# A narrower source for each packed tile's gather in a stack of four sparse graph attention layers

## The chip, the cores and the metric

The kernel runs on one core of one Trainium2 chip, as one launch. The metric is the device time of a launch in microseconds (us). TensorE (PE) multiplies matrices, VectorE (DVE) and ScalarE (ACT) do the elementwise work, GpSimd (POOL) issues the indirect DMAs, and SyncE (SP) issues the direct ones. Each engine works through its own queue in order; a semaphore makes an instruction wait for another engine or for a DMA.

## The reference, cut to what matters

There are 4096 nodes of 256 features and an adjacency matrix in which about one entry in 256 is set, besides the diagonal. Four graph attention layers follow one another, each with a residual and a layer norm:

```python
x = _layernorm(x + _L0_gnn_ref(x, adj, ...))   # 4 heads of 64
x = _layernorm(x + _L1_gnn_ref(x, adj, ...))   # 4 heads of 64
x = _layernorm(x + _L2_gnn_ref(x, adj, ...))   # 2 heads of 128
x = _layernorm(x + _L3_gnn_ref(x, adj, ...))   # 1 head, positive and negative attention
# within a layer, with h the projected nodes:
e = leaky_relu(s_src[i] + s_dst[j], 0.2)       # only where adj[i, j] is set
out[i] = sum_j softmax_j(e)[i, j] * h[j]
```

The sum over j has non-zero terms only for the neighbours of i.

## The kernel before, in words

**Packing.** The 4096 nodes are 32 row tiles of 128. The rows i of one tile m together have neighbours among some 40% of all nodes, so the kernel doesn't go through all 32 column tiles. It packs the nodes j that any row of tile m needs into 13 packed tiles of 128 (NG = 13, L71), in rising order of j. The tile's own 128 nodes come in addition, unpacked, as the seventh of 14 positions (FRONT = 6, L78; NP, L72). Nodes of the first 17 column tiles (MIX, L77) are laid from the front, the others from the back end. `windows()` (L101-122) computes, from the mean and 4.5 standard deviations of the number of touched nodes, which packed tiles a column tile j can reach: WINDOW[m, j] is a first packed tile and a number. If a node falls outside of that, a flag is set and a dense program computes everything (L165-168); with these inputs it isn't entered.

`Program.lists` (L285-475) makes the lists, while layer 0 already runs: `prepare` reads the adjacency (4 MB per block of four row tiles) and makes bytes of it, `places` computes each node's place, and `pack` (L416-451) moves, by one-hot matmuls (L436), the masks and the node numbers to their places. L448 to L451 compose the node number of each packed place from three digits, clip it, and write it to `idx[:, m, t]`: 128 node numbers of packed tile t of row tile m.

**Layers.** `Projection` (L520-591) computes, for one row tile of the next layer, the rows that the neighbours will need (values of all heads and attention terms) and stores them to DRAM as 128 rows of `vals` (L574). Each layer has a `vals` of its own with 4096 rows. `RowTile.load` (L614-631) fetches what one row tile of a layer needs, in two halves of seven positions: the own rows by a direct DMA (L626), each of the 13 packed tiles by an indirect DMA on POOL (L629), which takes 128 rows of `vals` by the numbers in `idx`. The buffers of these rows (`G`) come from a pool of 16 slots, two positions to a slot (one in layer 3, whose second halves have 14 slots of their own). `RowTile.half` (L633-682) then computes the attention weights `w` on ACT (L670, L657) and DVE (L666, L667, L671) and multiplies on PE (L679, L682). In layers 2 and 3 the last 3 and 1 blocks of four row tiles are computed unpacked, over all 32 column tiles (`whole_rows`, L866-919; PE L911).

**Order.** The order is written out by hand: `run` (L478-517), `Layer.part`, `half_alone`, `half_with_whole` and `close` (L744-863). A layer loads the first halves of its tiles 0 to 3 while the one before ends, and then the second half of tile 0. The waits aren't written out: the framework makes a gather wait for those stores whose rows lie in the slice of `vals` that the gather names as its source. L79 sets that slice: for the first six packed tiles (t below FRONT) it is the first 17 x 128 rows, for the other seven it is all 4096.

Of the kernel before, what the change touches and what calls it, by code (L numbers as in the profile page):

```python
# [37 lines left out]
F32 = mybir.dt.float32  # L38
# [7 lines left out]
ALU = mybir.AluOpType  # L46
# [4 lines left out]
P = 128  # L51
N = 4096
# [18 lines left out]
NG = 13  # L71
# [4 lines left out]
LEAD = 10  # L76
MIX = 17  # L77
FRONT = 6  # L78
NODES = tuple(MIX * P if t < FRONT else N for t in range(NG))  # L79
MC = P + 4  # L80
EDGE = 64.0
HEADS = (4, 4, 2, 2)
# [18 lines left out]
def windows():  # L101

    share = 1.0 - (1.0 - 1.0 / 256.0) ** P
    mean, sd = P * share, (P * share * (1.0 - share)) ** 0.5
    dev = 4.5
    out = {}
    for m in range(NT):
        for j in range(NT):
            if j == m:
                continue  # L110
            if j < MIX:
                n = sum(q != m for q in range(j))
                lo = mean * n - dev * sd * n ** 0.5
                hi = mean * (n + 1) + dev * sd * (n + 1) ** 0.5
            else:
                n = sum(q != m for q in range(j, NT))
                lo = CAP - mean * n - dev * sd * n ** 0.5
                hi = CAP - mean * (n - 1) + dev * sd * (n - 1) ** 0.5
            a = max(0, int(lo // P))
            b = min(NG - 1, int((hi - 1) // P))  # L120
            out[m, j] = (a, b - a + 1)
    return out


WINDOW = windows()
assert all(a >= FRONT for (m, j), (a, _) in WINDOW.items() if j >= MIX)
WMAX = max(n for _, n in WINDOW.values()) * P


# [57 lines left out]
class Program:  # L187
# [97 lines left out]
    def lists(self, ctx):  # L285


        tc, nc, ins, shared = self.tc, self.nc, self.ins, self.shared

        def pool(name, bufs):  # L290
            return ctx.enter_context(tc.tile_pool(name=name, bufs=bufs))

        cst, rawp, mkp, ohp = pool("icst", 1), pool("raw", 4), pool("imk", 2), pool("oh", 8)
        wk, cmp_ = pool("iwk", 2), pool("cm", 3)


        iotaI = wk.tile([P, WMAX], I32, name="iotaI", bufs=1)
        nc.gpsimd.iota(iotaI, pattern=[[1, WMAX]], base=1, channel_multiplier=0)
        iota = cst.tile([P, WMAX], F16, name="iota")
        nc.vector.tensor_copy(iota, iotaI)  # L300
# [39 lines left out]
        for j in range(NT):  # L340
            m = 0
            while m < NT:
                if m == j:
                    m += 1
                    continue
                e = m
                while e < NT and e != j and WINDOW[e, j] == WINDOW[m, j]:
                    e += 1
                a, n = WINDOW[m, j]
                nc.gpsimd.memset(lo[:, m:e, j], a * P - 1.0 - (CAP if j >= MIX else 0))  # L350
                nc.gpsimd.memset(wid[:, m:e, j], float(n * P))
                m = e
        total = cst.tile([P, NT], F32, name="total")
        bad = cst.tile([P, BT, NT], F32, name="bad")
        nc.vector.memset(bad, 0.0)

        class Block:
# [58 lines left out]
            def pack(self, it):  # L416
                m, mk = self.blk * BT + it, self.mk
                cm = cmp_.tile([P, NP, P], U8, name="cm")
                nc.scalar.copy(cm[:, FRONT, :], mk[:, m, it, :P])
                order = [j for j in range(NT) if j != m]  # L420
                touches = {}
                for j in order:
                    a, n = WINDOW[m, j]
                    for k in range(a, a + n):
                        touches.setdefault(k // 3, []).append((j, k))
                accs = {}
                for j in order:
                    a, n = WINDOW[m, j]
                    oh = ohp.tile([P, WMAX], BF16, name="oh")
                    nc.vector.tensor_scalar(oh[:, :n * P], iota[:, :n * P], self.place[:, it, j:j + 1], None,  # L430
                                            op0=ALU.is_equal)
                    for k in range(a, a + n):
                        b, s = divmod(k, 3)
                        if b not in accs:
                            accs[b] = prog.bank(prog.pfour)
                        nc.tensor.matmul(accs[b][:, s * MC:(s + 1) * MC], oh[:, (k - a) * P:(k - a + 1) * P],  # L436
                                         mk[:, j, it, :].bitcast(FP8), start=touches[b][0] == (j, k),
                                         stop=touches[b][-1] == (j, k), skip_group_check=True)
                        if touches[b][-1] == (j, k):
                            e = min(3, NG - 3 * b)  # L440
                            got = accs[b][:, :e * MC].rearrange("p (s c) -> p s c", c=MC)
                            o = 3 * b + (3 * b >= FRONT)
                            nc.scalar.activation(cm[:, o:o + e, :], got[:, :, :P], AF.Copy, scale=EDGE / 2.0)  # L443
                            nc.scalar.copy(self.num[:, it, 3 * b:3 * b + e, :], got[:, :, P:])
                nc.sync.dma_start(out=shared["maskC"][m], in_=cm)
                num = self.num[:, it]
                t = wk.tile([P, NG], F32, name="t")
                nc.vector.scalar_tensor_tensor(t, num[:, :, 0], 16.0, num[:, :, 1], op0=ALU.mult, op1=ALU.add)  # L448
                nc.vector.scalar_tensor_tensor(t, t, 16.0, num[:, :, 2], op0=ALU.mult, op1=ALU.add)
                nc.vector.tensor_scalar(shared["idx"][:, m, :FRONT], t[:, :FRONT], float(MIX * P - 1), None, op0=ALU.min)  # L450
                nc.vector.tensor_scalar(shared["idx"][:, m, FRONT:], t[:, FRONT:], float(N - 1), None, op0=ALU.min)  # L451

        prog = self
        block = Block(0)
# [23 lines left out]
    def run(self):  # L478
# [3 lines left out]
        with ExitStack() as ctx:  # L482
            lists = self.lists(ctx)
            xs = []
            for q in range(NT // 2):
                slot = self.g0.tile([P, 2 * ROW[0]], F32, name="G")
                nc.sync.dma_start(out=slot[:, :2 * F].rearrange("p (t f) -> p t f", t=2),
                                  in_=to_tiles(ins["x"][2 * q * P:2 * (q + 1) * P, :]))
                xs += [slot[:, :F], slot[:, F:2 * F]]

            line = [Projection(self, 0, w0, x, m, (self.ptwo[0], self.ptwo[1], self.pfour))
                    for m, x in enumerate(xs)]
            turns, listed = NT + 5, 0
            for m in range(turns):
                while listed < BT + LEAD and listed * turns <= m * (BT + LEAD):
                    next(lists)
                    listed += 1
                for k, step in enumerate(Projection.STEPS):
                    if 0 <= m - k < NT:
                        step(line[m - k])  # L500

            for m in range(NT):
                layer.part(m, 0)
                if m + LEAD < NT:
                    next(lists)
                layer.part(m, 1)
            for _ in lists:
                pass
# [11 lines left out]
class Projection:  # L520
# [68 lines left out]
    def all(self):  # L589
        for step in self.STEPS:  # L590
            step(self)


class RowTile:
# [19 lines left out]
    def load(self, half):  # L614
        L, m, n = self.layer, self.m, self.layer.n
        prog, nc, sh = L.prog, L.nc, L.shared
        if half == 0:
            self.S = prog.ld.tile([P, H4, P], F32, name="S")
            nc.sync.dma_start(out=self.S[:, :TERMS[n]], in_=sh["e"][n][m].partition_broadcast(P))
            self.mk = prog.ld.tile([P, NP, P], U8, name="mk")  # L620
            nc.sync.dma_start(out=self.mk, in_=sh["maskC"][m])
        else:
            self.y = L.load_x(m)
        for pos in range(HALF * half, HALF * (half + 1)):
            if pos == FRONT:
                nc.sync.dma_start(out=self.place(pos), in_=sh["v"][n][m * P:(m + 1) * P, :])  # L626
                continue
            t = pos - (pos > FRONT)
            nc.gpsimd.indirect_dma_start(  # L629
                out=self.place(pos), out_offset=None, in_=sh["v"][n][:NODES[t], :],  # L630
                in_offset=bass.IndirectOffsetOnAxis(ap=sh["idx"][:, m, t:t + 1], axis=0))

    def half(self, half):  # L633
# [824 lines left out]
```

## Time and profile before

The median of three runs is 2346.93 us (2338.59 to 2347.44). The profiled execution spans 2346.8 us, at a mean granted TensorE clock of 0.950.

| engine | busy us | share of span | instructions |
|---|---|---|---|
| PE | 2052.4 | 87% | 15689 |
| DVE | 1838.1 | 78% | 6100 |
| ACT | 1747.3 | 74% | 5137 |
| POOL | 1582.6 | 67% | 1596 |

Busy time is a sum over stages that are bound differently, so the shares alone don't tell what the end waits for. The chain of work that ended last is 47% PE, 20% DVE, 18% DMA and 8% ACT; its largest lines are PE L679 (17%) and L682 (12%) and the landing of gathers (12%). By the gathers, layer 0 runs from 101 us (first gather) to 812, layer 1 to about 1350, layer 2 to about 1780 and layer 3 to the end. In the lines of the profile, "G<-vals,idx" is a gather, "vals<-row" the store of a tile of rows, and the bracket at the end of a timeline line gives the idle time ahead of an instruction and the event that ended it, as far as the profile can infer it.

### The profile page before, as it was taken

The numbers are of one execution on the slowest core, as the hardware profiler recorded it, in microseconds if no ns is written. First come the engines' busy times: TensorE is split into PE (matmuls) and PEld (weight loads), VectorE is DVE, ScalarE is ACT, GpSimd is POOL, SyncE is SP. The second block draws the span as 40 slices with busy tenths as digits, with TensorE's granted clock in tenths as the row PEclk, the third lists the DMA queues.
The fourth block names the chain that finished last, engine by engine and source line by source line (L and its number), as shares of the span: only waits on it lengthen the run. The fifth ranks groups of instructions, "written<-read, shape, count | busy, mean of one in ns | idle before, by whom it ended". The sixth has DMA issues, their size and how long they took to land.

```text
span 2346.8 us, 49828 instructions
## 1 busy us (share of the span) xinstructions
PE 2052.4 (87%) x15689; PEld 1864.7 (79%) x15689; DVE 1838.1 (78%) x6100; ACT 1747.3 (74%) x5137; POOL 1582.6 (67%) x1596
## 2 busy tenths in 40 slices
PE   4878898989988769999999889889898799979996
PEld 3668788888888759988888879888887688868885
DVE  3889999999987759989899859876866365656567
ACT  4779898897787749988888859877663666666663
POOL 2127887777788757777777767755553677777773
PEclk7999999999999979999999989999999899989998
DMA  8889687775555556666666657666665788888883
GB/s 278 267 269 322 220 284 255 245 268 155 157 140 159 148 168 182 190 176 170 174 175 183 167 147 202 200 187 188 187 179 150 248 250 276 268 245 267 272 251 119
DMA packets 250325, 492.01 MB, mean 210 GB/s; under 512 B 44385, under 2 KB 156610, under 8 KB 249666
## 3 DMA queue, kind: packets, MB, share of 16 engines
q0 software_dynamic: 81536, 245.30, 37.1%
q1 hardware_dynamic: 168514, 243.42, 32.5%
q8 instruction: 126, 2.06, 0.4%
q14 instruction: 149, 1.22, 0.2%
HBM read 436.24 MB, written 52.31 MB: 208 GB/s over the span
## 4 chain that ended last, share of the span: by engine, by line
PE 47%; DVE 20%; DMA 18%; ACT 8%; issue 4%; POOL 3%; SPq 0%; ACTq 0%; DVEq 0%; POOLq 0%
PE bank L679 17%; PE bank L682 12%; DMA G<-vals,idx 12%; PE bank L911 7%; PE bank L546 5%; DVE w L671 5%; PE bank L436 4%; DMA G<-vals 3%; POOL G L629 3%; DVE w L666 3%; DVE w L667 3%; ACT w L670 3%; DVE oh L430 2%; DMA raw<-in_adjB_dram 2%; ACT pw L900 1%
## 5 line engine op out<-in xcount | busy, mean ns | idle before, releaser
L629 POOL DMA_INDIRECT G<-vals,idx x1456 | 1569.6, 1078 | 718.5 <-issue 188.1
L670 ACT ACTIVATE w<-S,G 128x128 f32<-128x128 f32 x3248 | 1009.6, 391 | 204.7 <-DMA G<-vals,idx 194.6
L679 PE MATMUL bank<-w,G 128*65 128x128 f32 x7168 | 846.8, 279 | 94.9 <-DVE w L667 65.0
L679 PEld LDWEIGHTS bank<-w,G 128*65 128x65 f32 x7168 | 810.4, 142 | 109.8 <-DVE w L667 84.5
L682 PE MATMUL bank<-G,w 128*128 128x257 f32 (+1 forms) x2688 | 499.4, 344 | 34.8 <-ACT z L970 11.5
L682 PEld LDWEIGHTS bank<-G,w 128*128 128x128 f32 x2688 | 439.2, 196 | 84.7 <-ACT z L970 13.9
L671 DVE SCALAR_TENSOR_TENSOR w<-w,mk 128x896 f32<-128x896 f32 x272 | 292.6, 1082 | 42.8 <-ACT w L670 42.1
L911 PE MATMUL bank<-vw,pw 128*128 128x129 f32 (+1 forms) x2048 | 304.8, 306 | 14.3 <-ACT zw L970 13.0
L911 PEld LDWEIGHTS bank<-vw,pw 128*128 128x128 f32 x2048 | 279.4, 195 | 32.0 <-ACT zw L970 13.4
L666 DVE TENSOR_SCALAR w<-S,G 128x128 f32<-128x128 f32 x896 | 238.7, 298 | 80.0 <-DMA G<-vals,idx 78.9
L657 ACT ACTIVATE w<-S,G 128x128 f32<-128x128 f32 x392 | 137.9, 389 | 146.6 <-DMA G<-vals 96.6
L546 PE MATMUL bank<-wext,xT 128*128 128x268 f32 (+3 forms) x640 | 188.3, 427 | 49.7 <-ACT xT L537 45.9
L430 DVE TENSOR_SCALAR oh<-iota,place 128x256 bf16<-128x256 f16 (+2 forms) x992 | 223.7, 298 | 8.3 <-PE bank L436 7.9
L671 DVE SCALAR_TENSOR_TENSOR w<-w,bank 128x896 f32<-128x896 f32 x192 | 206.0, 1078 | 8.9 <-ACT w L670 8.8
L436 PE MATMUL bank<-mk,oh 128*128 128x132 fp8e4 x2336 | 188.7, 228 | 15.7 <-DVE oh L430 8.7
L436 PEld LDWEIGHTS <-oh 128*128 128x128 bf16 x2336 | 147.3, 100 | 51.3 <-DVE oh L430 23.5
L546 PEld LDWEIGHTS bank<-wext,xT 128*128 128x128 f32 x640 | 122.0, 208 | 72.8 <-ACT xT L537 50.8
L908 DVE TENSOR_TENSOR pw<-pw,mw 128x512 f32<-128x512 f32 x64 | 43.9, 690 | 137.8 <-ACT pw L907 71.2
L901 DVE SCALAR_TENSOR_TENSOR pw<-pw,mw 128x512 f32<-128x512 f32 x192 | 127.8, 687 | 21.2 <-ACT pw L900 19.8
L373 ACT ACTIVATE mk<-raw 128x1024 uint8<-128x1024 int32 x128 | 131.5, 1063 | 16.9 <-DMA raw<-in_adjB_dram 16.5
L900 ACT ACTIVATE pw<-Sw,d 128x512 f32<-128x512 f32 x192 | 132.9, 708 | 3.4 <-PE bank L911 3.2
L443 ACT ACTIVATE cm<-bank 128x384 uint8<-128x384 f32 (+1 forms) x160 | 70.1, 451 | 60.4 <-PE bank L436 58.4
(131 smaller groups left out, 1710.5 us busy)
## 6 DMA issues: line engine op xcount, KB each, us to landing
raw<-in_adjB_dram SPq DMA_DIRECT2D x128, 512.0 KB
mk<-maskC SPq DMA_DIRECT2D x112, 224.0 KB
G<-vals,idx POOLq DMA_INDIRECT x1456
S<-edge SPq DMA_DIRECT2D x64, 256.0 KB
vw<-vals SPq DMA_DIRECT2D x96, 129.0 KB
xp<-y SPq DMA_DIRECT2D x96, 128.0 KB
y<-xp SPq DMA_DIRECT2D x96, 128.0 KB
mw<-maskW SPq DMA_DIRECT2D x20, 528.0 KB
```

The source lines that it names most:

```text
L430: nc.vector.tensor_scalar(oh[:, :n * P], iota[:, :n * P], self.place[:, it, j:j + 1], None, op0=ALU.is_equal)
L436: nc.tensor.matmul(accs[b][:, s * MC:(s + 1) * MC], oh[:, (k - a) * P:(k - a + 1) * P], mk[:, j, it, :].bitcast(FP8), start=touches[b][0] ...
L546: nc.tensor.matmul(pp[:, :c1 - c0], self.xT[:, k, :], wext[:, k, c0:c1], start=(k == 0), stop=(k == KT - 1 and brow is None))
L629: nc.gpsimd.indirect_dma_start(out=self.place(pos), out_offset=None, in_=sh["v"][n][:NODES[t], :], in_offset=bass.IndirectOffsetOnAxis(ap= ...
L657: nc.scalar.activation(w[0][:, k, :], S[:, 0, :], AF.Relu, bias=d(k, 0))
L666: nc.vector.tensor_scalar(w[h][:, k, :], S[:, h, :], d(k, h), LEAST, op0=ALU.mult, op1=ALU.max)
L670: nc.scalar.activation(w[h][:, k, :], S[:, h, :], AF.Exp, bias=d(k, h))
L671: nc.vector.scalar_tensor_tensor(w[h], w[h], LEAST, mh, op0=ALU.max, op1=ALU.mult)
L679: nc.tensor.matmul(accs[0][:Wd, h * P:(h + 1) * P], v, w[h][:, k, :], **how)
L682: nc.tensor.matmul(a, w[h][:, k, :], v, **how)
L900: nc.scalar.activation(p, S[:, h], AF.Exp, bias=d)
L911: nc.tensor.matmul(accs[it][:, c:c + Wd], p[:, it, :], v[:, c:c + Wd], start=(j == 0 and h == heads[0]), stop=(j == NT - 1), skip_group_ch ...
```

## The change

The slice that a gather names as its source is narrowed to what its packed tile can hold. From the same windows, REACH[t] is one more than the last column tile that can reach packed tile t. The gather of t names only the first REACH[t] x 128 rows of `vals`, so the framework makes it wait only for the stores of those rows. The node numbers are clipped to the same bounds: one instruction with a row of limits takes the place of two with constants. The limits are 13 memsets of one column each at the start.

```diff
--- before.py
+++ after.py
@@ -76,7 +76,6 @@
 LEAD = 10
 MIX = 17
 FRONT = 6
-NODES = tuple(MIX * P if t < FRONT else N for t in range(NG))
 MC = P + 4
 EDGE = 64.0
 HEADS = (4, 4, 2, 2)
@@ -124,6 +123,9 @@
 
 WINDOW = windows()
 assert all(a >= FRONT for (m, j), (a, _) in WINDOW.items() if j >= MIX)
+
+REACH = tuple(1 + max(j for (m, j), (a, n) in WINDOW.items() if a <= t < a + n) for t in range(NG))
+assert all(REACH[t] <= MIX for t in range(FRONT))
 WMAX = max(n for _, n in WINDOW.values()) * P
 
 
@@ -350,6 +352,9 @@
                 nc.gpsimd.memset(lo[:, m:e, j], a * P - 1.0 - (CAP if j >= MIX else 0))
                 nc.gpsimd.memset(wid[:, m:e, j], float(n * P))
                 m = e
+        limit = cst.tile([P, NG], F32, name="limit")
+        for t in range(NG):
+            nc.gpsimd.memset(limit[:, t:t + 1], REACH[t] * P - 1.0)
         total = cst.tile([P, NT], F32, name="total")
         bad = cst.tile([P, BT, NT], F32, name="bad")
         nc.vector.memset(bad, 0.0)
@@ -447,8 +452,7 @@
                 t = wk.tile([P, NG], F32, name="t")
                 nc.vector.scalar_tensor_tensor(t, num[:, :, 0], 16.0, num[:, :, 1], op0=ALU.mult, op1=ALU.add)
                 nc.vector.scalar_tensor_tensor(t, t, 16.0, num[:, :, 2], op0=ALU.mult, op1=ALU.add)
-                nc.vector.tensor_scalar(shared["idx"][:, m, :FRONT], t[:, :FRONT], float(MIX * P - 1), None, op0=ALU.min)
-                nc.vector.tensor_scalar(shared["idx"][:, m, FRONT:], t[:, FRONT:], float(N - 1), None, op0=ALU.min)
+                nc.vector.tensor_tensor(shared["idx"][:, m, :], t, limit, op=ALU.min)
 
         prog = self
         block = Block(0)
@@ -627,7 +631,7 @@
                 continue
             t = pos - (pos > FRONT)
             nc.gpsimd.indirect_dma_start(
-                out=self.place(pos), out_offset=None, in_=sh["v"][n][:NODES[t], :],
+                out=self.place(pos), out_offset=None, in_=sh["v"][n][:REACH[t] * P, :],
                 in_offset=bass.IndirectOffsetOnAxis(ap=sh["idx"][:, m, t:t + 1], axis=0))
 
     def half(self, half):
```

## The prediction

> **What bounds the kernel now.** I first read the costliest groups of the page, then the list of who waited for whom, because the change touches one instruction only, the gather of L629 on POOL.
>
> ```profile
> L629 POOL DMA_INDIRECT G<-vals,idx x1456 | 1569.6, 1078 | 718.5 <-issue 188.1
> ...
> POOL G L629 <- PE bank L532: 79.9, 6, 78.4
> POOL G L629 <- DVE oh L430: 58.5, 31, 49.4
> POOL G L629 <- ACT row L564: 34.3, 7, 32.5
> POOL G L629 <- DMA ablk<-in_a_dram: 14.8, 1, 14.8
> POOL G L629 <- DMA vals<-row: 7.7, 1, 7.7
> ```
>
> There are 1456 gathers, 13 per row tile; one keeps POOL for about 0.95 us and another 0.30 us passes before the next. The last column of the wait lines is the longest single wait: five of the names stand for one long wait each. The names themselves are guesses of the profile. The timeline of POOL dates these waits.
>
> ```profile
> 109.09 0.94 POOL L629 DMA_INDIRECT G<-vals,idx  x1 [0.30 <-issue]
> 159.43 1.01 POOL L629 DMA_INDIRECT G<-vals,idx  x1 [49.39 <-DVE oh L430]
> ...
> 842.39 0.94 POOL L629 DMA_INDIRECT G<-vals,idx  x1 [0.30 <-issue]
> 858.10 0.94 POOL L629 DMA_INDIRECT G<-vals,idx  x1 [14.76 <-DMA ablk<-in_a_dram]
> ...
> 1381.60 0.95 POOL L629 DMA_INDIRECT G<-vals,idx  x1 [0.30 <-issue]
> 1390.25 1.08 POOL L629 DMA_INDIRECT G<-vals,idx  x1 [7.70 <-DMA vals<-row]
> ...
> 1811.63 0.94 POOL L629 DMA_INDIRECT G<-vals,idx  x1 [32.51 <-ACT row L564]
> ```
>
> Between 159 and 1382, apart from 858, no POOL wait is over 4.3 us. So POOL's queue runs almost without a break and stops at the four places where a layer takes over from the one before. The stores of value rows on the DMA queue say what it waits for:
>
> ```profile
> 155.97 0.34 SPq L574 DMA_DIRECT2D vals<-row  x1
> ...
> 855.44 0.32 SPq L574 DMA_DIRECT2D vals<-row  x1
> ...
> 1387.33 0.32 SPq L574 DMA_DIRECT2D vals<-row  x1
> ...
> 1807.46 0.32 SPq L574 DMA_DIRECT2D vals<-row  x1
> ```
>
> The first three are the last row (31) of layers 0, 1 and 2, each 2.7 to 3.5 us ahead of the gather: the seventh gather of tile 0, the first with all of vals as its source. The fourth is row 16 of layer 3, by the order in which layer 2 finishes its rows; there the first gather waits, which names 17 rows. So waits follow the named rows.
>
> Whether POOL matters in a stage is read from busy time by stage (PE, PEld, DVE, ACT, POOL):
>
> ```profile
> 400.00:560.00 160.00, 146.34 (x1478) 132.08 (x1475) 159.80 (x547) 141.93 (x460) 118.83 (x95) 1.00 0.74 242
> 858.00:870.00 12.00, 0.11 (x1) 0.12 (x2) 3.31 (x9) 5.23 (x17) 9.16 (x10) 0.50 0.54 140
> 980.00:1340.00 360.00, 332.06 (x2772) 309.90 (x2772) 325.84 (x1038) 306.37 (x1026) 272.86 (x287) 0.98 0.64 175
> 1876.00:2300.00 424.00, 400.42 (x1800) 347.20 (x1800) 251.14 (x749) 273.44 (x587) 322.55 (x313) 0.97 0.85 261
> ```
>
> Layer 0 to 560 is full on DVE. At 858 to 870 PE does nothing: all wait for gathers. From 980 to 1340 POOL is full once its gaps are counted (272.9 + 287 x 0.30 = 359 of 360 us). Layer 3 is nearly full on both PE (400 of 424) and POOL (322.6 + 313 x 0.30 = 416).
>
> **What the Trainium skill says.** "Perfetto Trace Analysis", section "Per-instruction lifecycle", DMA Instruction - SWDGE: such an instruction waits for its semaphores before it runs, and its profiled end is the end of descriptor generation, not of the data movement. The trace agrees: the gather issued at 167.82 is busy for 1.93 us and its data release DVE only at 174.59. "SBUF - State Buffer", section "SBUF: two separate sides", says that DVE in some modes locks GpSimd out and so delays descriptors. This fits gathers of mean 1.25 us in layer 0 against 0.96 us in layer 1, but no run here isolates it.
>
> **The change part by part.** From the source's windows the numbers of row tiles named become 5, 8, 11, 13, 16, 17, 19, 21, 24, 26, 28, 31, 32 for gathers t = 0 to 12, in place of 17 (t below 6) and 32. Bytes and number of gathers stay.
>
> *Start of layer 0.* idx of tile 0 is ready at 67; rows are stored from 29 to 156. With 2 to 4.6 us for a store to land, gathers t = 6 to 11 can go at about 105, 115, 128, 135, 143 and 157; only t = 12 waits until 159.4. Tile 1 follows six gathers earlier: 167.82 - 159.43 = 8.4 us for POOL. The consumer gains less, for DVE has other work until 169.3 and is idle then:
>
> ```profile
> 170.20 0.29 DVE L666 TENSOR_SCALAR w<-S,G 128x128 f32<-128x128 f32 x1 [0.86 <-DMA G<-vals,idx]
> 171.07 0.28 DVE L666 TENSOR_SCALAR w<-S,G 128x128 f32<-128x128 f32 x1 [0.59 <-DMA G<-vals,idx]
> 172.25 0.28 DVE L666 TENSOR_SCALAR w<-S,G 128x128 f32<-128x128 f32 x1 [0.89 <-DMA G<-vals,idx]
> 174.59 0.29 DVE L666 TENSOR_SCALAR w<-S,G 128x128 f32<-128x128 f32 x1 [2.06 <-DMA G<-vals,idx]
> ```
>
> 0.86 + 0.59 + 0.89 + 2.06 = **4.4 us** (bounds 2 and 8.4). DVE is full afterwards, so this is kept; POOL's larger lead is given back where it waits for buffers (407, 473, 559).
>
> *Layer 0 to 1.* POOL is idle 14.8 us; t = 6 to 10 need rows long stored, and t = 11 needs row 30, stored at 849.3. All six are issued in the idle time, and only t = 12 waits until 858.1: 6 x 1.25 = 7.5 us. Tile 0's data are complete at 858.1 + 4.4 = 862.5 (the landing time of the gather at 858.10) instead of 868.4, which is 5.9 us earlier; tile 2's second half may then wait about 1.3 us for a buffer. I take **6 us** (4 to 7.5). DVE and ACT are full until 980 and POOL after it; all of them start earlier, so nothing gives it back.
>
> *Layer 1 to 2.* The wait of 7.7 us holds the same six gathers, 7.5 us. PE is busy until 1397 with whole-row matmuls, then idle until 1402.2 for tile 0's second half; tile 1's data are complete at 1410.7 and would be at 1403. **5.5 us** (3 to 7.5).
>
> *Layer 2 to 3.* t = 0 to 3 need rows under 13, t = 4 row 15 (stored at 1782.7): five gathers move out of the queue behind 1811.6, into an idle wait of 32.5 us; t = 5 still needs row 16. 5 x 1.25 = 6.25 us. ACT's waits for gathers from 1814 to 1831 sum to 8.0 us, so it can use them. The next POOL wait, at 1845.5, is for a buffer that PE frees when it ends tile 1's first half, and moves along. **5.5 us** (3 to 7), kept to the end since layer 3 is bound by POOL and PE in turn.
>
> *The clip.* 64 small DVE instructions (L450, L451) become 32; a tensor_tensor of such a size costs like L448 (183 ns), of which pipelining leaves some 0.08 us as the distance to the next one. About 22 of the 32 packs fall in the DVE-bound stretch: 22 x 0.08 = 1.8, I take **1 us** saved (0 to 2.4). Thirteen memsets of one column, like those of L350 (0.4 us, 0.05 to 0.1 us apart), come at 23 us, when POOL has nothing to do until 67: nothing.
>
> *Added waits.* A gather that is the first to need new rows waits for them itself; behind it stand only the later gathers, which in the queue of before waited as long or longer. A wait instruction of the DMA queue takes 17 ns at the median (semaphore entries beside L574); 31 rows in four layers would make 31 x 4 x 17 ns = 2 us, nearly all of it in POOL's idle waits: nothing.
>
> Sum: 4.4 + 6 + 5.5 + 5.5 + 1 = 22.4 us; 2346.9 - 22.4 = **2324.5 us**.
>
> **Rivals.** (A) *Half is absorbed.* Buffers limit how far POOL may run ahead, and the DMA engines are full at 165 to 180 (400 GB/s), so a later wait can take the place of the one removed. For: POOL stalls for buffers in layer 0 and again from 1517 to 1757. Against: at 858 to 870 and 1850 to 1865 all engines stand still for gathers. Only layers 0 to 1 and 2 to 3 pay, at their low bounds, with 2 us at the start: 4 + 3 + 2 = 9, so 2338. (B) *All of POOL's time counts:* 8.4 + 7.5 + 7.5 + 6.3 + 2 = 31.7, so 2315. For: POOL alone is full in half the program. Against: DVE is full until 560, which cuts the first term. (C) *Slower.* The order within engines is not the program's (row projections stand among matmuls of a tile at 844 to 852), so something schedules by dependences; fewer dependences can reorder ACT and PE, and early gathers take 0.8 MB (6 x 134 KB, the size of a stored tile of rows) of bandwidth from the adjacency loads, which stand in the chain from 90 to 157. A loss of about 5 us per layer would exceed the gain: 2365. Against: POOL's own order can hardly change, and 0.8 MB is 3 us at 270 GB/s, given back at 160.
>
> **How the numbers follow.** Forecast (2318 to 2333) 0.52, A 0.22, B 0.13, C 0.13. The range runs from all upper bounds, 2314, up to 2345, which takes in A and leaves out C and a little at each end. Faster by over 0.5% is under 2335.2: forecast and B whole, and a quarter of A, 0.70; within 0.5%: the rest of A and a part of C, 0.20; slower 0.10.
>
> **What would show it.** After the change: no single POOL wait of 49 us at 159 but several, with one gather of tile 0 left behind the last; the wait at 843 split, ending in t = 12; DVE's four waits at 170 gone; PE's idle at 858 to 870 shorter by some 6 us; five gathers before 1800 in the turn to layer 3. If gathers still wait for row 31 at t = 6, dependences are kept coarser than the named rows and nothing is gained. If POOL's waits for buffers grow by what was saved, A is right. If the order on ACT or PE differs, C can be.

## The result, and the profile after

The changed kernel takes 2365.2 us at the median of four runs (2363.9 to 2371.7); the kernel before took 2342.8 us beside it (2337.3 to 2347.4). The ratio is 1.0102, with a 95% interval of 1.0068 to 1.0136: it is **slower by 1%**, where 2324.5 us was forecast. The profiled execution spans 2362.1 us at a granted clock of 0.948 (before: 2346.8 us at 0.950); a clock 0.2% lower doesn't make 1%. Busy times hardly move: PE 2055.8 us against 2052.4, ACT 1750.6 against 1747.3, DVE 1838.1 in both.

First, what the change was made for. This is POOL's timeline at the start of layer 0 in the changed kernel (start, duration, then in brackets the idle time ahead and what ended it). All line numbers from L126 on are up to five higher than before: the gather is L633, the exponential of the weights L674 (L670 before).

```profile
69.72 1.25 POOL L633 DMA_INDIRECT G<-vals,idx  x1 [46.61 <-DVE oh L435]
...
120.43 0.94 POOL L633 DMA_INDIRECT G<-vals,idx  x1 [11.67 <-PE bank L441]
132.49 0.94 POOL L633 DMA_INDIRECT G<-vals,idx  x1 [11.11 <-DMA vals<-row]
140.34 1.08 POOL L633 DMA_INDIRECT G<-vals,idx  x1 [6.90 <-PE bank L441]
148.20 0.95 POOL L633 DMA_INDIRECT G<-vals,idx  x1 [6.78 <-DMA vals<-row]
162.35 1.15 POOL L633 DMA_INDIRECT G<-vals,idx  x1 [13.21 <-DMA vals<-row]
163.80 0.95 POOL L633 DMA_INDIRECT G<-vals,idx  x1 [0.30 <-DVE oh L435]
```

In place of the long waits that ended at 101 (78.4 us) and at 159 (49.4 us) there are one to 69.72 and ten of 4 to 13 us, each ahead of the gather of one packed tile. The last two gathers of tile 0, which need rows 30 and 31, go at 162.35 and 163.80. DVE's four waits at 170 to 175, which the prediction counted, are gone. This part did what it was meant to.

Now the turns between layers. The same view, at the turn from layer 0 to 1, from 1 to 2 and from 2 to 3:

```profile
857.60 0.95 POOL L633 DMA_INDIRECT G<-vals,idx  x1 [5.72 <-ACT w L674]
...
868.88 0.94 POOL L633 DMA_INDIRECT G<-vals,idx  x1 [3.05 <-DMA vals<-row]
...
880.39 0.94 POOL L633 DMA_INDIRECT G<-vals,idx  x1 [9.31 <-ACT w L674]
...
1406.99 0.94 POOL L633 DMA_INDIRECT G<-vals,idx  x1 [10.46 <-DMA vals<-row]
...
1416.63 0.98 POOL L633 DMA_INDIRECT G<-vals,idx  x1 [2.36 <-DMA vals<-row]
...
1424.38 1.78 POOL L633 DMA_INDIRECT G<-vals,idx  x1 [5.51 <-ACT w L674]
...
1803.45 0.95 POOL L633 DMA_INDIRECT G<-vals,idx  x1 [0.30 <-ACT row L568]
...
1839.44 0.94 POOL L633 DMA_INDIRECT G<-vals,idx  x1 [26.03 <-ACT row L568]
```

The wait for stored rows at the turn from 1 to 2 did not shrink from its 7.7 us: it is 10.5 us, comes 17 us later than in the kernel before (1406.99 against 1390.25), and 2.4 us more follow ahead of the one gather of tile 0 that needs the last row. The stores say the same. These are the stores of the last rows (31) that layers 0, 1 and 2 gather:

```profile
160.64 0.32 SPq L578 DMA_DIRECT2D vals<-row  x1
...
865.38 0.33 SPq L578 DMA_DIRECT2D vals<-row  x1
...
1413.75 0.32 SPq L578 DMA_DIRECT2D vals<-row  x1
```

Before, these stood at 155.97, 855.44 and 1387.33. **The rows that everything waits for are stored later than before: by 10 us at the turn from layer 0 to 1, and by 26 us at the turn from 1 to 2.** (The 5 us of the first are not the change's: in full_b, a second set of runs of the same kernel, this store comes at 155.72, and in the kernels of the same clock below whose layer 0 names the rows of before, between 157.01 and 161.94.) So it is not enough to ask what a gather waits for; the question is what now delays the rows. ACT's timeline at the turn from layer 1 to 2 answers it. L568 and L588 are steps by which a last row of values and its terms come to be; L674 is an exponential for a tile of layer 2.

```profile
1377.12 0.15 ACT L568 ACTIVATE row<-bank 128x2 f32<-128x2 f32 x1
1394.76 0.69 ACT L674 ACTIVATE w<-S,G 128x128 f32<-128x128 f32 x2 [17.49 <-DMA G<-vals,idx]
1395.84 0.40 ACT L674 ACTIVATE w<-S,G 128x128 f32<-128x128 f32 x1 [0.39 <-DMA G<-vals,idx]
1397.09 0.69 ACT L674 ACTIVATE w<-S,G 128x128 f32<-128x128 f32 x2 [0.85 <-DMA G<-vals,idx]
1397.69 0.34 ACT L588 ACTIVATE erow<-bank,shift 2x128 f32<-2x128 f32 x1
...
1403.36 0.17 ACT L568 ACTIVATE row<-bank 128x2 f32<-128x2 f32 x1 [1.61 <-PE bank L553]
```

ACT stands still for 17.5 us, for a gather of a second half. That gather waits for nothing but its turn: POOL issues one each 1.25 us without a break through this stretch. Behind the waiting exponential, in ACT's own queue, stand the steps of the last two rows (30 and 31) that layer 2 gathers. PE and DVE then wait for ACT, PE for the copy of row 30 (L541) and DVE for its L568, and nearly everything stands still (the columns of the last line are busy time of PE, PEld, DVE, ACT and POOL, then the granted clock, the DMA share and GB/s):

```profile
1400.04 2.11 PE L550 MATMUL bank<-wext,xT 128*128 128x262 f32 x4 [17.83 <-ACT xT L541]
...
1403.57 0.16 DVE L570 COPY row<-bank 128x4 f32<-128x4 f32 x1 [20.72 <-ACT row L568]
...
1382.50:1394.70 12.20, 0.00 (x0) 0.00 (x0) 0.31 (x2) 0.00 (x0) 9.15 (x11) 0.59 0.40 106
```

In the kernel before, such an exponential could not go ahead of the last row: its gather named all rows, so by its dependences it came after them. There the last rows' steps (L564 is L568 above) come first, and PE, with the matmuls over all column tiles (L911) among others, is full in the same stretch:

```profile
1386.50 0.17 ACT L564 ACTIVATE row<-bank 128x2 f32<-128x2 f32 x1 [1.87 <-PE bank L549]
...
1393.99 0.40 ACT L670 ACTIVATE w<-S,G 128x128 f32<-128x128 f32 x1 [1.13 <-DMA G<-vals,idx]
...
1382.50:1394.70 12.20, 12.10 (x96) 10.88 (x95) 5.96 (x15) 6.06 (x12) 3.58 (x5) 1.00 0.44 129
```

In the table, the layers by their gathers in the two profiles (end is the issue of the layer's last gather, by count in POOL's order):

| | before: ends at | after: ends at | after - before | change within the layer |
|---|---|---|---|---|
| layer 0 | 811.1 | 809.7 | -1.5 | -1.5 |
| layer 1 | 1349.4 | 1353.4 | +4.0 | +5.5 |
| layer 2 | 1778.2 | 1802.2 | +24.0 | +20.0 |
| layer 3 | 2310.0 | 2330.7 | +20.7 | -3.3 |
| end | 2346.8 | 2362.1 | +15.3 | -5.4 |

Layer 2 alone is more than the whole loss. The loss seems to grow through layer 2 if one follows gathers, but this is only POOL's lead over the other engines shrinking: by ACT's instructions the delay of 20 us is complete at the turn (shown below).

### The profile page after: what moved, and what is told of

The parts are those of the page before. It is cut to its first block, busy times and chain, and to the rows that moved or that the text cites. A ratio compares the mean times of both kernels' runs of the same rounds, so it can differ in the third digit from the quotient of the medians.

```text
span 2362.1 us, 49805 instructions
## 1 busy us (share of the span) xinstructions
PE 2055.8 (87%) x15689; PEld 1863.8 (79%) x15689; DVE 1838.1 (78%) x6068; ACT 1750.6 (74%) x5137; POOL 1587.8 (67%) x1609
## 4 chain that ended last, share of the span: by engine, by line
PE 44%; DMA 21%; DVE 20%; ACT 7%; issue 5%; POOL 3%; SPq 0%; POOLq 0%; DVEq 0%; ACTq 0%
DMA G<-vals,idx 14%; PE bank L683 14%; PE bank L686 14%; PE bank L915 7%; DVE w L675 5%; PE bank L441 4%; PE bank L550 4%; POOL G L633 3%; DVE w L670 3%; DMA raw<-in_adjB_dram 3%; DVE w L671 3%; DMA G<-vals 3%; ACT w L674 2%; DVE oh L435 2%; ACT pw L904 1%
## 5 line engine op out<-in xcount | busy, mean ns | idle before, releaser
L633 POOL DMA_INDIRECT G<-vals,idx x1456 | 1574.5, 1081 | 734.1 <-issue 180.2
L674 ACT ACTIVATE w<-S,G 128x128 f32<-128x128 f32 x3248 | 1015.1, 392 | 242.7 <-DMA G<-vals,idx 223.2
L670 DVE TENSOR_SCALAR w<-S,G 128x128 f32<-128x128 f32 x896 | 237.3, 297 | 77.1 <-DMA G<-vals,idx 75.4
```

Of the source, the lines that this page charges most:

```text
L633: nc.gpsimd.indirect_dma_start(out=self.place(pos), out_offset=None, in_=sh["v"][n][:REACH[t] * P, :], in_offset=bass.IndirectOffsetOnAxis ...
L670: nc.vector.tensor_scalar(w[h][:, k, :], S[:, h, :], d(k, h), LEAST, op0=ALU.mult, op1=ALU.max)
L674: nc.scalar.activation(w[h][:, k, :], S[:, h, :], AF.Exp, bias=d(k, h))
```

## The experiments

The theory, called Q in the expectations, is that the order of the queues, built by dependences, has changed, and work that waits for late gathers stands ahead of the last rows. Its main rival, W, is that the narrower transfers are slower in themselves or collide with something; another, P, that the order of POOL's queue alone does the harm.

All ratios are to the kernel before, run in the same set on the same chip. In the first and the last set the kernel before took 2836 and 2838 us, at a granted clock near 0.87; in the three others 2346 to 2347 us at 0.95. The absolute times expected in the first set were for 0.95.

**The parts.** One helper takes the place of the slice that a gather names; the tensor of limits stays in all of them. `clip` has an empty list of layers (all gathers as before), `n1` layer 1, `n2` layer 2, `n03` layers 0 and 3.

```diff
+    def named(n, t):
+        if n in (2,):
+            return REACH[t] * P
+        return MIX * P if t < FRONT else N
...
-                out=self.place(pos), out_offset=None, in_=sh["v"][n][:REACH[t] * P, :],
+                out=self.place(pos), out_offset=None, in_=sh["v"][n][:self.named(n, t), :],
```

**The extra.** `gate12` has all of the change, and in layers 1 and 2 makes the weights of tile 0's second half wait for the last gather of that half (t = 12, the one that needs row 31), by columns that DVE copies from it and the weights then overwrite. The expectations call it the last gather of the tile's first half, which is a slip: in `half`, `G` holds the seven positions of the half at work. It takes no transfer away and leaves the gathers as early as they are; it forbids an order in which those exponentials stand ahead of the last rows.

```diff
         w = [prog.wp.tile([P, HALF, P], F32, name="w") for _ in range(H)]
+        if self.m == 0 and half == 1 and n in (1, 2):
+            for h in range(H):
+                nc.vector.tensor_copy(w[h][:, :, 0], G[HALF - 1][:, :HALF])
```

First set (clock 0.87):

clip: 

> The clip alone: node numbers clipped by the row of limits in one instruction, every gather names its source as before (17 row tiles for t below 6, all 32 else). Theory (order): the loss of the full change comes from the turns of layer 0 to 1 and 1 to 2, where ACT's order has tile 0's second half ahead of the last projections; here the waits and those turns are as before, so the time is that of before within 5 us, 2338 to 2348. Rival (clip): the one changed instruction reorders the list making of layer 0, and the loss is here: 2355 or more.

n1: 

> The narrow source in layer 1 only, with the clip. Theory (order): row 31 of layer 1 is stored some 10 us later than before, relative to the turn, since the steps of its projection stand behind tile 0's activations on ACT; layer 1 as a whole takes 5 us longer: 2346 to 2352. Rival (my prediction's step: the six gathers that move into the idle time bring 6 us, and the loss comes from elsewhere): 2334 to 2340.

n2: 

> The narrow source in layer 2 only, with the clip. Theory (order): ACT stands still for about 17 us at the turn of layer 1 to 2 for a gather of tile 0's second half while the projections of rows 30 and 31 are queued behind it; layer 2 takes 15 to 20 us longer: 2357 to 2365. Rival (prediction's step, 5.5 us gained): 2335 to 2340.

gate12: 

> The full change, and in layers 1 and 2 a gate: for the second half of tile 0, VectorE first copies seven values of the last gathered rows (t = 12) into column 0 of each weight tile; the activations then overwrite them, so they can't be put ahead of the projection of row 31, which t = 12 waits for. The waits of the gathers are those of the full change. Theory (order on ACT): most of the loss goes, and what the early gathers bring shows: 2322 to 2342. Rival (the loss is from the waits or the traffic of the gathers themselves, or from the order on POOL, where other gathers stand ahead of t = 12): 2355 to 2368, like the full change.

Measured: clip 0.9974 (0.9952 to 0.9995), n1 0.9980 (0.9956 to 1.0004), n2 0.9988 (0.9962 to 1.0015), gate12 0.9943 (0.9922 to 0.9964). The first three can't be told apart from each other. The traces show the delay at this clock too, but the layer makes up for it: the last row of layer 2 is stored 67.5 us after the layer's first gather in n2 and 53.1 us after it in clip, yet from the first to the last gather the layer takes 480 us in both. The set settled nothing but that gate12 is faster than before there too.

Second set (clock 0.95):

full_b, the changed kernel itself: 

> The changed kernel itself, timed beside the three others on one chip. All expectations of this set are ratios to the kernel before[...]. Theory Q (the queue order built with the narrower sources puts work that waits for late gathers ahead of the last rows' chains between layers 0, 1 and 2): 1.010 where the clock is granted at 0.95; where it is at 0.87 the array is the bound nearly everywhere and the same order costs less, 0.999 to 1.004. Rival W (the narrower transfers themselves are slower, whatever the order): over 1.008 at either clock.

gate12_b, the same as gate12: 

> All of the change, and one small extra in layers 1 and 2: the first row tile's second half fills one column of each weight tile from the last gather of its first half before its weights are computed, so that the order cannot put that half's exponentials ahead of the last rows of the layer before. Theory Q: at least 0.008 of the changed kernel's ratio comes back at a clock of 0.95 (0.993 to 1.000), 0.003 to 0.006 below the changed kernel at 0.87. Rival W: within 0.002 of the changed kernel. Rival P (what hurts is the order on GpSimd alone, where the second row tile's gathers stand ahead of the first one's last): within 0.003 of the changed kernel, since GpSimd's order stays as the change makes it.

n03: 

> The narrower sources in layers 0 and 3 alone, where the order of the queues is hardly touched, and the tensor of limits; layers 1 and 2 name the rows they named before. Theory Q: faster, 0.994 to 0.998 at a clock of 0.95 (the start of layer 0 some 2 to 4 us, the boundary from layer 2 to 3 some 5 us), 0.995 to 0.999 at 0.87. Rival W: slower, over 1.003, since half of the gathers are narrow.

n2_b, the same as n2: 

> The narrower sources in layer 2 alone, and the tensor of limits. In the trace of the changed kernel layer 2 lost most, 20 us against before. Theory Q: slower at a clock of 0.95, 1.004 to 1.009; at 0.87 0.998 to 1.001. Rival W: 1.002 to 1.003, a quarter of the whole loss.

| kernel | median us | ratio | interval |
|---|---|---|---|
| full_b | 2369.0 | 1.0096 | 1.0066 to 1.0126 |
| gate12_b | 2339.2 | 0.9966 | 0.9952 to 0.9980 |
| n03 | 2344.8 | 0.9990 | 0.9973 to 1.0007 |
| n2_b | 2373.0 | 1.0108 | 1.0078 to 1.0137 |

W falls: gate12_b has every narrow transfer and is faster than before. P falls: with the extra, POOL's gathers stand one by one in the order of the changed kernel, and the time comes back all the same. n03 is less fast than theory Q had it; more on that below. And n2_b, with narrower sources in layer 2 alone, has the whole loss, more than either theory had said. In n2_b ACT's queue differs in one stretch from that of n0, a build (not timed) with the narrower sources in layer 0 alone and with all queues in the order of `clip`. The beginning of that stretch, where L680 is the exponential, L541, L568 and L588 the steps of the last rows:

```
 L588 Activation erow<-bank,shift_69 2x128
 L541 TensorCopy xT<-bank 128x256
+L680 Activation w<-S,G 128x128 x14
+L568 Activation row<-bank 128x2
+L680 Activation w<-S,G 128x128 x3
+L588 Activation erow<-bank,shift_69 2x128
 L680 Activation w<-S,G 128x128 x5
-L568 Activation row<-bank 128x2
-L588 Activation erow<-bank,shift_69 2x128
-L541 TensorCopy xT<-bank 128x256
-L568 Activation row<-bank 128x2
```

In the rows with a minus the last rows' steps follow one another; in those with a plus, exponentials stand between them. PE's and DVE's queues differ around this turn too, and no run changes ACT's alone; but in the trace of the changed kernel it is PE and DVE that wait for ACT there. ACT's timeline of n2_b shows what this costs:

```profile
1386.71 0.40 ACT L680 ACTIVATE w<-S,G 128x128 f32<-128x128 f32 x1 [13.48 <-DMA G<-vals,idx]
1387.01 0.15 ACT L568 ACTIVATE row<-bank 128x2 f32<-128x2 f32 x1
...
1401.75 0.17 ACT L568 ACTIVATE row<-bank 128x2 f32<-128x2 f32 x1 [1.25 <-PE bank L553]
```

In n03, whose layer 2 has the sources of before, the last rows' steps run without an exponential between them:

```profile
1377.70 0.17 ACT L568 ACTIVATE row<-bank 128x2 f32<-128x2 f32 x1 [1.88 <-PE bank L553]
1378.72 0.36 ACT L588 ACTIVATE erow<-bank,shift 2x128 f32<-2x128 f32 x1 [0.85 <-PE bank L582]
1379.67 0.37 ACT L541 COPY xT<-bank 128x256 f32<-128x256 f32 x1 [0.58 <-PE bank L536]
1381.91 0.17 ACT L568 ACTIVATE row<-bank 128x2 f32<-128x2 f32 x1 [1.87 <-PE bank L553]
```

Counted from the first gather of layer 2 in each (1346.6 and 1347.6), the last row's L568 comes 55.2 us later in n2_b and 34.3 us later in n03: **21 us at this turn.** In full_b it is 1407.48 - 1352.0 = 55.5 us, in gate12_b 1379.98 - 1345.2 = 34.8 us, and in the kernel before 1386.50 - 1350.6 = 35.9 us. The turn explains layer 2: the first of the `erow` steps of the next layer comes at 1456.68 in n2_b and at 1437.09 in n03, already 20 us apart, and the nineteenth, at 1727.30 and 1704.29, 23 us apart. So some 3 us at most are lost in the body of the layer.

Third set (clock 0.95). `gate2` is the extra in layer 2 alone (`n == 2`); `gatebefore` puts the extra into the kernel before.

gate2: 

> All of the change, with the small extra (the first row tile's second half waits for the last gather of its first half) in layer 2 alone. Theory Q2 (nearly the whole loss is the order on ScalarE at the boundary from layer 1 to 2, where the exponentials of the first tile's second half stand ahead of the last rows' values): at a clock of 0.95 it comes back from 1.010 to 0.996 to 1.001, at 0.87 within 0.002 of the kernel with the extra in layers 1 and 2. Rival Q1 (the boundary from 0 to 1 carries half of the loss): 1.003 to 1.006 at 0.95.

n1_b: 

> The narrower sources in layer 1 alone, and the tensor of limits. Theory Q2: 0.998 to 1.003 at a clock of 0.95, since this boundary lost 5 us in the trace of the changed kernel, of which some is the earlier start of that kernel given back. Rival Q1: 1.003 to 1.006.

clip_b: 

> The tensor of limits alone (one minimum for the two of before), with the rows of before named by every gather. Both theories: 0.998 to 1.001. A value under 0.997 would say that the gain of the narrow layers 0 and 3 is not theirs but that of the other order in the making of the lists.

gatebefore: 

> The kernel before, with the small extra in layers 1 and 2 and nothing of the change: a control for the extra itself. Theory Q2: 0.998 to 1.003, since in the kernel before no exponential of a second half can stand ahead of the last rows. Rival G (the extra is a gain in itself, whatever the sources): 0.990 to 0.997.

| kernel | median us | ratio | interval |
|---|---|---|---|
| gate2 | 2349.7 | 1.0017 | 1.0002 to 1.0033 |
| n1_b | 2358.1 | 1.0039 | 1.0023 to 1.0056 |
| clip_b | 2351.1 | 1.0023 | 1.0009 to 1.0037 |
| gatebefore | 2351.4 | 1.0027 | 1.0012 to 1.0041 |

The extra is no gain in itself: in the kernel before it measures 1.0027. In the changed kernel, with it in layer 2 alone, 1.0096 - 1.0017 = 0.0079 comes back (18.5 us of 2347), and the extra in layer 1 brings 1.0017 - 0.9966 = 0.0051 more (12 us). So both turns count, at something like 60 to 40; "nearly the whole" at the turn from 1 to 2 was too much. The turn from 0 to 1 shows the same picture in ACT's timeline of n1_b, in layer 1's exponentials and the rows' steps:

```profile
861.25 0.40 ACT L680 ACTIVATE w<-S,G 128x128 f32<-128x128 f32 x1 [4.48 <-DMA G<-vals,idx]
861.56 0.16 ACT L568 ACTIVATE row<-bank 128x4 f32<-128x4 f32 x1
...
865.19 0.24 ACT L574 ACTIVATE row<-bank,shift 128x2 f32<-128x2 f32 x1
...
875.05 0.25 ACT L574 ACTIVATE row<-bank,shift 128x2 f32<-128x2 f32 x1
```

The last row's L574 comes 53.1 us after the first gather of layer 1 here (821.9), against 41.3 us in clip_b (858.90 - 817.6) and 42.2 us in gate12_b (852.37 - 810.2).

Fourth set (clock 0.95). clip_b had been slower than expected. The single minimum had also changed the order in which the lists are made, on PE, DVE and ACT, so `clip2` takes the minimum in two instructions, after which the queues stand nearly as before:

```diff
-                nc.vector.tensor_tensor(shared["idx"][:, m, :], t, limit, op=ALU.min)
+                nc.vector.tensor_tensor(shared["idx"][:, m, :FRONT], t[:, :FRONT], limit[:, :FRONT], op=ALU.min)
+                nc.vector.tensor_tensor(shared["idx"][:, m, FRONT:], t[:, FRONT:], limit[:, FRONT:], op=ALU.min)
```

`full2` and `gate12t` are the changed kernel and gate12 with this; `best` has it with narrower sources in layers 0, 1 and 3 and the extra in layer 1 alone.

clip2: 

> The tensor of limits alone, but with the minimum taken in two instructions, for the same two groups of tiles as before: the queues then stand nearly in the order of the kernel before (28 lines of difference on ScalarE where the single minimum has 243). Theory S (what the single minimum costs is the other order in which the lists are made): 0.998 to 1.001. Rival T (the minimum against a tensor or the 13 fills of the limits cost it themselves): 1.002 to 1.004, as the single minimum measured.

full2: 

> All of the change with the minimum in two instructions. Theories S and Q2 together: the single minimum's 0.0023 comes off and the boundaries' loss stays, 1.005 to 1.009. Rival T: 1.009 to 1.012, unchanged. A value under 1.002 would say that the loss at the boundary from layer 1 to 2 is no property of the narrower sources but of this one order.

gate12t: 

> All of the change with the small extra in layers 1 and 2 and the minimum in two instructions. Theory S: 0.992 to 0.996, where the same kernel with one minimum measured 0.9966. Rival T: 0.996 to 0.998.

best: 

> The narrower sources in layers 0, 1 and 3, the small extra in layer 1 alone, layer 2 with the rows of before, and the minimum in two instructions. From the ratios measured so far: layers 0 and 3 take 0.0033 off, layer 1 with the extra 0.0034, layer 2 with the extra gave nothing: 0.991 to 0.995 by theory S, 0.994 to 0.997 by rival T.

| kernel | median us | ratio | interval |
|---|---|---|---|
| clip2 | 2348.6 | 1.0018 | 1.0003 to 1.0034 |
| full2 | 2366.3 | 1.0107 | 1.0082 to 1.0133 |
| gate12t | 2339.9 | 0.9977 | 0.9961 to 0.9992 |
| best | 2337.0 | 0.9966 | 0.9949 to 0.9983 |

Theory S falls: two instructions measure what one did, in all three pairs. So the order of the list-making makes no difference that these runs can see, and full2 shows the loss of the turns in a second build. best and gate12_b are the fastest, both by 0.34%. What narrower sources give in layer 2 behind the extra is too small to be seen: best, without them, is not slower than gate12t.

Last set (clock 0.87): `memonly` is the kernel before with the thirteen fills of the limits, not used; `same` is the kernel before.

memonly: 

> The kernel before with the thirteen fills of the tensor of limits on GpSimd added and nothing else: the tensor is filled and not used, the minimum is taken with the two numbers of before, and every queue stands in the order of before. If the fills cost what the tensor of limits alone measured: 1.0015 to 1.003. If it is the minimum against a tensor on VectorE, or the small rest of another order: 0.999 to 1.001.

same: 

> The kernel before once more, unchanged, as a measure of what such a ratio is worth: 0.999 to 1.001. A value of 1.0015 or more would say that the ratios near 1.002 of the tensor of limits and of the control tell nothing.

Measured: memonly 1.0010 (0.9982 to 1.0038), same 0.9981 (0.9954 to 1.0009). Inconclusive. The kernel before against itself comes out as far from 1 as the effect that was looked for. Whether the 0.002 of clip_b and clip2 is the fills, the minimum against a tensor or an uncertainty beyond their intervals stays open. It also means that clip, n1 and n2 of the first set show nothing; gate12's 0.9943 there is the only one clear of it.

## Why the prediction was wrong, point by point

Its sum is compared with the parts measured at clock 0.95, as shares of 2347 us. A difference of two ratios carries about 5 us of uncertainty (the two half intervals, 0.0014 and 0.0017, added as squares, give 0.0022), 8 us where n2_b is in it. The runs are from two sets, and what the sets themselves may add isn't in these figures.

| term | forecast | measured as | us |
|---|---|---|---|
| start of layer 0 and turn 2 to 3 | -4.4 - 5.5 = -9.9 | n03 - clip_b = -0.0033 | -8 |
| turn 0 to 1 | -6 | n1_b - clip_b = +0.0016 | +4 |
| turn 1 to 2 | -5.5 | n2_b - clip_b = +0.0085 | +20 |
| limits | -1 | clip_b = +0.0023 | +5 |
| sum | -22.4 | +0.0091 (full_b: +0.0096) | +21 |

**Start of layer 0 and turn 2 to 3: right in sum.** The forecast of the two together lies within the uncertainty; they weren't measured apart. At the start of layer 0 no queue changes its order in the build (n0 against `clip`), and the last gather of tile 0 follows the store of the last row after 3.2 us where it took 11.9: 8.7 us, where the prediction gave POOL 8.4. At the turn to layer 3 ACT's order does change, in the same way as at the other turns: in n03, weights of layer 3 (L667) stand ahead of the last rows' steps.

```profile
1782.44 0.40 ACT L667 ACTIVATE w<-S,G 128x128 f32<-128x128 f32 x1 [1.17 <-DMA G<-vals,idx]
1782.74 0.34 ACT L588 ACTIVATE erow<-bank,zero 1x128 f32<-1x128 f32 x1
1782.99 0.34 ACT L541 COPY xT<-bank 128x256 f32<-128x256 f32 x1
1785.01 0.40 ACT L667 ACTIVATE w<-S,G 128x128 f32<-128x128 f32 x1 [1.67 <-DMA G<-vals,idx]
```

Here the waits are 1 to 2 us, where the other was 17.5, since the gathers are the first of their layer and none stands before them. What they cost shows between the stores of rows 15 and 16 of that layer, 28.0 us apart in n03 (1780.38 and 1808.40) and 25.0 us in clip_b (1790.55 and 1815.58). At this clock it is 27.7 to 31.7 us in all eight traces with narrower sources in layer 3, and 24.4 to 26.4 us in the six without. So some 3 us of this turn's gain go the way of the other turns' loss, by the traces; no run takes just this out. That n03 as a whole is hardly faster than before (0.9990) fits the 1.0023 of the limits that it carries, as far as that figure holds.

**Turns 0 to 1 and 1 to 2: wrong, and this is the step that failed.** Under added waits the prediction said that behind a waiting gather "stand only the later gathers, which in the queue of before waited as long or longer", and added nothing. That looked at POOL's queue alone. The consumers of the early gathers are exponentials on ACT, and with fewer dependences these were placed ahead of the last rows' steps in ACT's queue. An engine works through its queue in order, so a 17.5 us wait for a gather that merely had its turn to wait for held up the rows, which all further gathers waited for. Then "all of them start earlier, so nothing gives it back" fails too. With the order protected, the 6 us at the turn from 0 to 1 fit what was measured: +0.0016 - 0.0051 = -0.0035, some -8 us with an uncertainty of 7, with the cost of the extra included. At the turn from 1 to 2, +0.0085 - 0.0079 leaves nothing, with an uncertainty of 11 us. There, by the trace of gate12_b, the extra itself can have taken the gain back, since no exponential of the second half can start before t = 12 has landed, and ACT waits 11 us for its copies (L657; the exponential is L677 here):

```profile
1381.94 5.02 ACT L907 ACTIVATE pw<-Sw,d 128x512 f32<-128x512 f32 x8 [0.58 <-PE bank L918]
1398.09 4.20 ACT L677 ACTIVATE w<-S,G 128x128 f32<-128x128 f32 x14 [11.13 <-DVE w L657]
```

The 5.5 us forecast there are therefore neither confirmed nor refuted: a way of keeping the order that lets the first of those exponentials start before that was not tried.

**The limits: mis-sized.** 1 us saved was forecast, from -2.4 to 0; measured is a loss of 2 to 9 us by clip_b's interval. The cause stays open, as said.

**The rivals.** C named the mechanism and the total: 2365 us, by an order on ACT and PE that fewer dependences change. That the total fits is in part luck, since C spread it as 5 us over every layer, and one turn alone carries 20. It was given 0.13, because "POOL's own order can hardly change". POOL's order did change, in a few places, but that was beside the point: with that order kept and ACT's mended, the kernel is faster than before. The 0.8 MB of early bandwidth, C's other leg, has no support: the last row of layer 0 is stored between 154.6 and 161.8 in the kernels with early gathers in that layer, no later than in those without. A and B fell with the step above.

**The signs.** The split of the wait at 159, the end of DVE's waits at 170 and the five early gathers of layer 3 came as said; two gathers of tile 0, not one, were left for the end of the wait. PE's busy time from 858 to 870 is 5.1 us where it was 0.1, which was one of the signs; but of the 30 us from 850 to 880 PE is busy for 15.6, where it was 14.5. **The gap had moved, not closed.** A sign of one fixed window was too easily met; the time at which the last row is stored would have told at once.

## What to carry to other kernels

A dependence that is wider than it need be may be holding the order of another engine's queue together. Before narrowing one, list the consumers of what becomes early, find the engine that they run on, and ask what stands behind them there. If it is the work that the narrowed transfers finally wait for, it waits as long as those consumers do: 17.5 us at one turn here turned the gain into a loss, and waits of 1 to 2 us at another took a part of it. Narrow it and keep the order by hand (0.9966), or leave it wide where the order can't be kept; and read the result at the producer, by when its last store is issued, not at the wait that was to shrink.

## What the runs showed of the hardware that was not expected

The same kernel took 2347 us in three sets and 2836 and 2838 us in two others, 21% more. The mean granted clock of the profiles was 0.95 and 0.87, 8% apart, so the clock as the records show it is not the whole of it. In the long profile (`same`, 2823.7 us) PE was busy for 2268.8 us against 2052.4, which is 80% of the span against 87%, so it doesn't bind nearly everywhere, as the expectation of full_b has it. The mean matmul of the layers' weights (L679) took 291 ns against 279, and that of the lists (L436) 258 ns against 228. This row of PE's groups in it shows idle time that the profile puts down to no other engine:

```profile
L679 PE MATMUL bank<-w,G 128*65 128x128 f32 x7168 | 949.1, 291 | 198.0 <-issue 158.3 <-DVE w L667 19.3 <-ACT w L670 17.1
```

Before, the same row had 94.9 us of idle time, none of it listed under "issue". What these idle times are was not tried. A change to a wait is worth less there: the changed orders that cost 1% at 0.95 could not be told from no change at 0.87 in n2.
